# Two transformer layers on one core: layer 1's normalized rows get the projection bias early, in GpSimd's queue, and its last stage is cut into five parts

## The chip, the core and the metric

One Trainium2 chip, one of its cores. A core has a matrix engine (PE; its weight loads are listed apart as PEld), a vector engine (DVE), a scalar engine (ACT), GpSimd (POOL) and a sync engine (SP), which here only issues DMAs. Each engine works through its own queue in order. The metric is device time of the program in microseconds (us), median of several executions.

## The reference

Input: x of 4 x 512 tokens, 512 wide, all in float32. Each of two layers computes `xn = layernorm(x)` and then `x + attention(xn) + experts(xn)`. The change touches the expert part of layer 1:

```python
logits = x @ router_w + router_b            # x is xn here; 8 experts
vals, idx = top_k(logits, 2); w = softmax(vals)
h = x @ expert_w[e] + expert_b[e]           # for the two experts chosen
combined = sum over the two of w * silu(h)
out = combined @ proj_w + proj_b
y = x + out
return norm_w * y / sqrt(mean(y * y) + 1e-6)
```

So the last lines need, for each token, its normalized row plus the projection bias, `x + proj_b`. Layer 1's attention has 16 heads of width 32; its output is added to the same result.

## The kernel before, in words

The 2048 tokens are 16 tiles of 128 rows (`NT = 16`, four to a batch). Layer 0 is done first (to about 1450 us). Its normalization for layer 1 writes the normalized rows to DRAM (`xnd`) and keeps their transpose in SBUF (`xnT`).

**Order of the work.** The kernel is written for a scheduler that traces the program, assumes a time for every instruction, and puts each engine's instructions into a queue by readiness and by their place in the program. `tc.keep_in_program_order(ins)` ties an instruction behind the one traced before it on its engine. The queue that results is fixed: on the chip an instruction whose input is late holds up all that stand behind it.

**Layer 1** runs over 16 groups of four heads (`NG`), each with four key blocks, so 64 steps, `at[0]` to `at[63]`. Each step does the scores (`st`, L1241), their exponential on ACT (`pT`, L1243), the context (`cx`, L1255) and the running sum over keys on DVE (`pS`, L1261). Queries and keys (`qp`), values (`vp`), inverses (`rsum`) and the output projection (`o`, L1324, added to the result on DVE at L1313) are spread over the steps. PSUM has three banks for all `mm` products, and a bank is free again once its reader (mostly DVE) is done.

**Experts among the steps.** After the routing, a list `jobs1` (L1393 to L1434) hangs further work on steps. Within a step the jobs run in the order of the list.
- From step 9: `begin_experts1`, then 36 expert tiles. Each fetches rows (`xr`), one or two sets of weights (`we`, every third into part of `acc`) and a bias (`be`) by indirect DMAs from GpSimd's queue, all in `load` (L478 to L482). A tile is transposed (`trm`, L517) and multiplied (`hp`, L529); its result goes to DRAM (`yd`).
- Step 48: `begin_mixing` gives the experts' SBUF back, opens the pool of the last stage and loads `pw`, `pb`, `nw1`.
- Steps 48 to 63, per token tile n, four parts on successive steps. `mix`: two indirect gathers (`row0`, `row1`, L545), a load of the normalized rows (`xa`, L1354), the first weighting on DVE (L1357), the second with the sum on DVE (L1358), and the bias added on GpSimd (L1359). `turn_mix`: four transposes (`trc`, L1366), ACT's copy (`combT`, L1370). `project_mix`: four products (`po`, L1377), the sum on DVE (L1378), the squares on ACT (`ysq`, L1381), two tiny operations on GpSimd (`yss`, L1382 and L1383). `finish_mix`: scaling on DVE (L1388) and the addition to the result (L1313), then the store.
- Pools of the last stage hold two buffers of each kind.

**At the seam of the layers** (L1436 to L1454) the first values (`vp`), layer 1's last four normalizations (`norm`, `trx`) and the router's logits (`lg`, copied to SBUF as `lr` by ACT, transposed as `trg`) are traced in alternation.

## Time and profile before

| what | value |
|---|---|
| median of 3 runs | 2068.45 us (2067.59 to 2068.87) |
| the profiled execution | 2068.36 us |
| its span, first to last instruction | 2066.3 us |
| PE busy | 2014.5 us, 97% of the span |
| DVE, ACT, POOL busy | 1450.5, 868.2, 753.6 us |
| granted PE clock, mean | 0.996 |
| PE busy in 1560 to 1872 us (expert tiles) | 312.00 of 312.00 us |
| PE busy in 1889 to 2041 us (last stage) | 144.09 of 152.00 us |

The profile is of one execution. The time is 2.06 us more than its span. A line of the timeline gives start, duration, engine, line, operation, output and inputs, shape, count, and in brackets the idle time before it with what ended that time. "Releaser" is the event that came last.

### The profile page before, as it was taken

The page shows a single profiled execution, that of the slowest core. Times are in us where ns is not written, and L with a number is a line of the kernel's source. Part 1 is how long each engine was busy: PE and PEld are TensorE (multiplying, and loading weights), DVE is VectorE, ACT ScalarE, POOL GpSimd, SP SyncE. Part 2 cuts the span into 40 slices and gives each one's busy share as a digit, 9 for nine tenths or more (in the row PEclk, how much of TensorE's full clock was granted, in tenths as well). Part 3 has the DMA queues.
Part 4 walks back from the last instruction along what each step waited for, and adds up shares of the span by engine and source line. Part 5 has one row for each costly group of instructions (what it writes and reads, how often), then busy time and mean ns, then how long its engine had stood idle before and what let it go on. Part 6 is the DMA issues. An engine that isn't in the chain of part 4 may idle for free.

```text
span 2066.3 us, 27983 instructions
## 1 busy us (share of the span) xinstructions
PE 2014.5 (97%) x9130; PEld 1202.9 (58%) x9130; DVE 1450.5 (70%) x3543; ACT 868.2 (42%) x2600; POOL 753.6 (36%) x761
## 2 busy tenths in 40 slices
PE   7999999999999999999999999999999999999998
PEld 4666666666666666666666666666334445445442
DVE  7888967666666766676667778787596555557775
ACT  4554444444444444443444454454243432333332
POOL 4422244443323333344343444353114332332550
PEclk9999999999999999999999999999999999999999
DMA  7111134323332342235443222121317765773551
GB/s 250 68 37 57 42 128 137 123 101 113 139 120 98 118 145 103 95 134 180 182 160 116 72 81 78 42 72 62 120 51 246 262 244 191 262 240 129 155 161 58
DMA packets 98907, 267.23 MB, mean 129 GB/s; under 512 B 14401, under 2 KB 27841, under 8 KB 87489
## 3 DMA queue, kind: packets, MB, share of 16 engines
q0 software_dynamic: 27072, 148.91, 21.2%
q1 hardware_dynamic: 70528, 114.34, 16.3%
q10 hardware_dynamic: 1152, 2.10, 0.3%
q8 instruction: 75, 1.23, 0.2%
q14 instruction: 80, 0.65, 0.1%
HBM read 222.05 MB, written 42.73 MB: 128 GB/s over the span
## 4 chain that ended last, share of the span: by engine, by line
PE 81%; DVE 8%; ACT 3%; POOL 2%; issue 2%; DMA 1%; ACTq 0%; DVEq 0%; POOLq 0%
PE p L675 24%; PE hp_r L529 12%; PE op L842 10%; PE st L767 4%; PE qp L1217 3%; PE st L1241 3%; PE sp L758 3%; PE cx L1255 2%; PE ca L811 2%; PE trm_r L517 2%; PE o L1324 1%; DVE pS L1261 1%; PE trq L695 1%; PE vp L1177 1%; PE cc L814 1%
## 5 line engine op out<-in xcount | busy, mean ns | idle before, releaser
L842 PE MATMUL op<-Wo,cT 128*128 128x512 f32 x512 | 230.4, 598 | 5.3 <-DVE lv L739 2.9
L529 PE MATMUL hp_r<-we_r,xT_r 128*128 128x512 f32 (+1 forms) x592 | 224.7, 596 | 0.0
L481 POOL DMA_INDIRECT xr_r<-xnd,rows_r x72 | 89.4, 1241 | 331.1 <-PE trm_r L517 297.8
L775 POOL TENSOR_TENSOR lT<-lT,lmask 128x512 f32<-128x512 f32 (+1 forms) x128 | 157.9, 1247 | 140.2 <-ACT lT L771 140.0
L675 PE MATMUL p<-wT,x 128*128 128x384 f32 x512 | 179.8, 494 | 0.8 <-DVE wT L119 0.8
L675 PE MATMUL p<-wB,x 128*128 128x384 f32 x512 | 176.2, 488 | 4.0 <-DVE u L731 4.0
L675 PE MATMUL p<-wA,xnT 128*128 128x384 f32 x512 | 173.3, 491 | 0.2 <-DVE u L710 0.2
L842 PEld LDWEIGHTS op<-Wo,cT 128*128 128x128 f32 x512 | 92.0, 190 | 114.7 <-issue 77.9
L575 ACT ACTIVATE sq<-qb 128x128 f32<-128x128 f32 x384 | 118.9, 310 | 93.9 <-DVE qb L724 45.6
L1243 ACT ACTIVATE pT<-st 128x1024 f32<-128x1024 f32 x128 | 123.7, 1014 | 62.7 <-PE st L1241 57.0
L529 PEld LDWEIGHTS hp_r<-we_r,xT_r 128*128 128x128 f32 (+1 forms) x592 | 83.0, 170 | 97.9 <-issue 92.5
L845 DVE TENSOR_TENSOR acc<-acc,op 128x512 f32<-128x512 f32 x128 | 87.4, 685 | 68.9 <-PE op L842 68.5
L675 PEld LDWEIGHTS p<-wB,x 128*128 128x128 f32 x512 | 93.7, 190 | 68.2 <-issue 9.9
L675 PEld LDWEIGHTS p<-wT,x 128*128 128x128 f32 x512 | 94.5, 193 | 63.5 <-issue 6.3
L675 PEld LDWEIGHTS p<-wA,xnT 128*128 128x128 f32 x512 | 95.3, 192 | 60.7 <-issue 2.6
L689 ACT ACTIVATE qb<-qb,ss 128x128 f32<-128x128 f32 x256 | 81.9, 390 | 106.4 <-POOL ss L578 103.3
L519 ACT COPY xT_r<-trm_r 128x512 f32<-128x512 f32 x72 | 41.8, 581 | 197.5 <-PE hp_r L529 187.6
L771 ACT ACTIVATE lT<-st,ss 128x256 f32<-128x256 f32 (+1 forms) x128 | 47.0, 448 | 174.9 <-PE st L767 174.8
L767 PE MATMUL st<-qkT 128*128 128x256 f32 (+1 forms) x512 | 109.0, 353 | 1.5 <-ACT qkT L702 1.5
L545 POOL DMA_INDIRECT row_r<-yd,slot_r x64 | 74.2, 1160 | 95.0 <-DVE row_r L1358 36.7
L767 PEld LDWEIGHTS st<-qkT 128*128 128x128 f32 x512 | 92.0, 191 | 12.8 <-ACT qkT L702 1.7
L578 POOL TENSOR_TENSOR ss<-ss,nhalf 128x6 f32<-128x6 f32 x64 | 96.1, 1501 | 5.3
(360 smaller groups left out, 4330.9 us busy)
## 6 DMA issues: line engine op xcount, KB each, us to landing
x<-xsd SPq DMA_DIRECT2D x112, 256.0 KB, 3.0
yd<-yr_r SPq DMA_DIRECT2D x72, 256.0 KB, 3.5
wA<-in_wA SPq DMA_DIRECT2D x16, 384.0 KB, 3.6
wB<-in_wB SPq DMA_DIRECT2D x16, 384.0 KB, 7.6
xnd<-xn SPq DMA_DIRECT2D x24, 256.0 KB, 2.0
accd<-acc SPq DMA_DIRECT2D x18, 256.0 KB, 2.0
acc<-in_x SPq DMA_DIRECT2D x16, 256.0 KB, 5.8
Wo<-in_Wo SPq DMA_DIRECT2D x8, 512.0 KB, 3.7
```

What stands on the lines that cost most here:

```text
L481: G.indirect_dma_start(out=out, out_offset=None, in_=src, in_offset=at_rows(idx))
L529: PE.matmul(hp[ts(h, m), :], lhsT=xT[:, k, ts(h, m)], rhs=w[:, ts(k, HID)], start=(k == 0), stop=(k == KC - 1))
L545: G.indirect_dma_start(out=x, out_offset=None, in_=self.yd, in_offset=at_rows(self.r.slot[:, k, n : n + 1]))
L575: A.activation(sq, x[:, h, :], AF.Square, accum_out=ss[:, h : h + 1])
L578: pin(G.tensor_tensor(ss, ss, nhalf[:, 0:n], ALU.pow))
L675: PE.matmul(p, lhsT=x[:, k, ts(c, P)], rhs=w[:, k, :], start=(k == 0), stop=(k == 1))
L689: A.activation(x[:, j, :], x[:, j, :], AF.Copy, scale=sq[t][:, j : j + 1])
L767: PE.matmul(st[:, ds((t % 2) * 256, n)], lhsT=qkT[:, HG + h, ts(t, P)], rhs=qkT[:, h, ds(t * P, n)], start=True, stop=True)
L775: G.tensor_tensor(dst, dst, lmask.rearrange("p a w j -> p (a w j)")[:, 0:n], ALU.mult)
L842: PE.matmul(op, lhsT=cT[:, h, ts(t, P)], rhs=wo[:, h, :], start=(h == 0), stop=(h == HG - 1))
L845: V.tensor_tensor(acc[:, n, :], acc[:, n, :], op, ALU.add)
L1243: A.activation(pt[:, ts(pair, 2), :], st, AF.Exp, scale=SCALE1)
```

## The change

In four parts.

1. **Normalized rows plus bias** (`xpd`, a new DRAM array). At step 9 the projection bias is loaded into the row that held layer 1's output bias, no longer needed (`load_bias`). For each of the 16 token tiles, GpSimd's queue loads `xnd`'s rows (step 14 + 2n), and one step later adds the bias and stores the sum to `xpd`. The buffer `xp` is single. These, and all indirect loads of layer 1's experts, are tied to program order.
2. **The last stage in five parts.** `begin_mixing` moves from step 48 to step 47. The gathers become a part of their own (`gather_mix`), one step ahead of the weighting; `row0` gets three buffers, `row1` keeps two. `turn_mix` loads the finished `xpd` rows (four buffers) instead of `mix` loading `xnd` rows, and GpSimd's addition in the last stage is gone. The parts of the first tiles are kept from coming too early, so that tiles 0, 1 and 2 are turned one step later than before; the others on the same steps. The buffer of the squares becomes single.
3. **The first weighting** moves from DVE (a tensor_scalar) to ACT (a Copy activation with the gate as scale). The second, on DVE, is tied to program order for the first four tiles, and so is the last addition of `values7` for the last batch.
4. **At the seam**, the first two normalizations are traced ahead of the first values, and the logits and their transposes come one place earlier.

```diff
+    xpd = dram.tile([T, HID], F32, tag="xpd", name="xpd")
...
-            G.indirect_dma_start(out=out, out_offset=None, in_=src, in_offset=at_rows(idx))
+            pin = tc.keep_in_program_order if self.silu else (lambda x: x)
+            pin(G.indirect_dma_start(out=out, out_offset=None, in_=src, in_offset=at_rows(idx)))
...
+            if b + 1 == B:
+                tc.keep_in_program_order(last_)
...
+    def load_bias():
+        rows["pb"] = rout["wo_b"]
+        nc.sync.dma_start(out=rows["pb"], in_=a["pb"].partition_broadcast(P))
+    def fetch_normalized(n):
+        held["xp", n] = rout["ex1"].pool.tile([P, HID], F32, tag="xp", name=f"xp_{n}", bufs=1)
+        tc.keep_in_program_order(G.dma_start(out=held["xp", n], in_=xnd[ts(n, P), :]))
+    def add_bias(n):
+        x = held.pop(("xp", n))
+        tc.keep_in_program_order(G.tensor_tensor(x, x, rows["pb"], ALU.add))
+        tc.keep_in_program_order(G.dma_start(out=xpd[ts(n, P), :], in_=x))
...
+    def gather_mix(n):
+        held[n] = []
+        for k in range(2):
+            x = rout["mix"].tile([P, HID], F32, tag=f"row{k}", name=f"row{k}_r1_{n}", bufs=3 - k)
+            G.indirect_dma_start(out=x, out_offset=None, in_=yds[1], in_offset=at_rows(r1.slot[:, k, n : n + 1]))
+            held[n].append(x)
     def mix(n):
-        g0, g1 = rout["ex1"].gather(n)
-        x = rout["mix"].tile([P, HID], F32, tag="xr", name=f"xa_{n}")
-        nc.sync.dma_start(out=x, in_=xnd[ts(n, P), :])
-        pin = tc.keep_in_program_order if n < 2 else (lambda x: x)
-        pin(V.tensor_scalar(g0, g0, r1.gate[:, 0, n : n + 1], None, ALU.mult))
-        V.scalar_tensor_tensor(g0, g1, r1.gate[:, 1, n : n + 1], g0, ALU.mult, ALU.add)
-        G.tensor_tensor(x, x, rows["pb"], ALU.add)
+        g0, g1 = held[n]
+        A.activation(g0, g0, AF.Copy, scale=r1.gate[:, 0, n : n + 1])
+        weighed = V.scalar_tensor_tensor(g0, g1, r1.gate[:, 1, n : n + 1], g0, ALU.mult, ALU.add)
+        if n < TC:
+            tc.keep_in_program_order(weighed)
     def turn_mix(n):
-        g0, x = held[n]
+        g0, _ = held[n]
+        x = rout["mix"].tile([P, HID], F32, tag="xr", name=f"xa_{n}", bufs=4)
+        nc.sync.dma_start(out=x, in_=xpd[ts(n, P), :])
...
-    first += 6 + NS * 11 // 12
+    jobs1.append((at[first], load_bias))
+    for n in range(NT):
+        jobs1.append((at[first + 5 + 2 * n], lambda n=n: fetch_normalized(n)))
+        jobs1.append((at[first + 6 + 2 * n], lambda n=n: add_bias(n)))
+    first += 5 + NS * 11 // 12
     jobs1.append((at[first], begin_mixing))
     for n in range(NT):
         here = first + n * 13 // 16
-        for d, f in ((0, mix), (1, turn_mix), (2, project_mix), (3, finish_mix)):
-            jobs1.append((at[here + d], lambda n=n, f=f: f(n)))
+        for d, f in ((0, gather_mix), (1, mix), (2, turn_mix), (3, project_mix), (4, finish_mix)):
+            place = max(here + d, first + 1 + d + (n > 1)) if d else here
+            jobs1.append((at[place], lambda n=n, f=f: f(n)))
...
+    norm = [next_layer(3 * TC + t, rp, bank1) for t in range(2)]
     values(0, 0)
-    norm = [next_layer(3 * TC + t, rp, bank1) for t in range(2)]
     norm[0][0]()
+    turn_ = second_logits(B - 2, rp, bank1)
     values(0, 1)
-    turn_ = second_logits(B - 2, rp, bank1)
+    turn_()
     norm[0][1]()
     norm[1][0]()
     norm.append(next_layer(3 * TC + 2, rp, bank1))
     values(0, 2)
-    turn_()
```

More of the change, by code (lines that the diff above doesn't have):

```diff
@@ L1190, in values7 @@
             V.tensor_tensor(v[b][:, 2:4, h2], p5, u3, ALU.add)
-            V.tensor_tensor(v[b][:, 2:4, h1], product("p3", sv4, block(b, f2, 1)), u2, ALU.add)
+            last_ = V.tensor_tensor(v[b][:, 2:4, h1], product("p3", sv4, block(b, f2, 1)), u2, ALU.add)
+            if b + 1 == B:
+                tc.keep_in_program_order(last_)
     def queries(g, i):
@@ L1344, in begin_mixing @@
         rout["mix"] = scratch.enter_context(tc.tile_pool(name="mix", bufs=2, side="right"))
-        rout["ex1"].pool = rout["mix"]
         load_square(rout["mix"], "pw")
-        for nm in ("pb", "nw1"):
-            rows[nm] = load(rout["mix"], nm, [P, HID], a[nm].partition_broadcast(P))
-    def mix(n):
-        g0, g1 = rout["ex1"].gather(n)
-        x = rout["mix"].tile([P, HID], F32, tag="xr", name=f"xa_{n}")
-        nc.sync.dma_start(out=x, in_=xnd[ts(n, P), :])
-        pin = tc.keep_in_program_order if n < 2 else (lambda x: x)
-        pin(V.tensor_scalar(g0, g0, r1.gate[:, 0, n : n + 1], None, ALU.mult))
-        V.scalar_tensor_tensor(g0, g1, r1.gate[:, 1, n : n + 1], g0, ALU.mult, ALU.add)
-        G.tensor_tensor(x, x, rows["pb"], ALU.add)
-        held[n] = g0, x
+        rows["nw1"] = load(rout["mix"], "nw1", [P, HID], a["nw1"].partition_broadcast(P))
+    def gather_mix(n):
[4 more added lines that the diff above has]
+            held[n].append(x)
+    def mix(n):
+        g0, g1 = held[n]
[3 more added lines that the diff above has]
+            tc.keep_in_program_order(weighed)
     def turn_mix(n):
-        g0, x = held[n]
+        g0, _ = held[n]
+        x = rout["mix"].tile([P, HID], F32, tag="xr", name=f"xa_{n}", bufs=4)
+        nc.sync.dma_start(out=x, in_=xpd[ts(n, P), :])
         tr = bank1("mm", f"trc_{n}")
@@ L1378, in project_mix @@
         V.tensor_tensor(y, y, op, ALU.add)
-        sq = rout["mix"].tile([P, HID], F32, tag="th", name=f"ysq_{n}")
+        sq = rout["mix"].tile([P, HID], F32, tag="th", name=f"ysq_{n}", bufs=1)
         ss = small.tile([P, 1], F32, tag="yss", name=f"yss_{n}")
```

## The prediction, made before the changed kernel was run

> **What bounds the kernel.** I read the page's busy times first. PE is busy 97% of the span, so a change off PE can only win what PE loses. The stages tell where that is.

> ```profile
> PE 2014.5 (97%) x9130; PEld 1202.9 (58%) x9130; DVE 1450.5 (70%) x3543; ACT 868.2 (42%) x2600; POOL 753.6 (36%) x761
> ```
> ```profile
> 1889.00:2041.00 152.00, 144.09 (x618) 64.17 (x616) 110.17 (x154) 55.90 (x96) 70.75 (x74) 0.99 0.42 127
> 1560.00:1872.00 312.00, 312.00 (x1391) 144.04 (x1389) 179.05 (x248) 112.53 (x166) 106.67 (x106) 1.00 0.70 237
> ```

> The lines by window give a stretch, its length and the busy time of PE, PEld, DVE, ACT and POOL, then clock, DMA share and GB/s. Among the expert tiles (1560 to 1872) PE never pauses: work put there is free while its cover lasts, and nothing can be won there. In the last stage PE loses 7.9 us. Where, PE's timeline says:

> ```profile
> 1955.95 3.70 PE L1324 MATMUL o<-woT,cT 128*128 128x512 f32 x8 [0.25 <-DVE xa L1378]
> 1960.12 3.67 PE L1377 MATMUL po<-pw,combT 128*128 128x512 f32 x8 [0.48 <-DVE xa L1378]
> 1968.31 3.53 PE L1217 MATMUL qp<-xnT,wqT 128*128 128x256 f32 x8 [2.01 <-DVE xnT L1313]
> ...
> 2003.29 3.67 PE L1377 MATMUL po<-pw,combT 128*128 128x512 f32 x8 [0.42 <-DVE xa L1378]
> 2011.52 3.67 PE L1377 MATMUL po<-pw,combT 128*128 128x512 f32 x8 [2.05 <-DVE acc L1313]
> 2019.30 3.67 PE L1377 MATMUL po<-pw,combT 128*128 128x512 f32 x8 [0.75 <-DVE xa L1378]
> 2029.50 2.04 PE L1241 MATMUL st<-qk 32*128 32x512 f32 x8 [0.40 <-ACT pT L1243]
> ```

> In all but the last PE waits for DVE to empty a PSUM bank: DVE sets the pace in bursts, though it is busy only 110 of 152 us. Behind the 2.01 us pause the qp products run slowly: the chain of waits gives these 16 products 5.42 us, and 3.65 us elsewhere. The windows show a granted clock of 0.93 in 1960 to 1985, so 0.07 x 25 = 1.75 us of clock are lost there. DVE's and POOL's timelines show why DVE is late:

> ```profile
> 1963.17 0.48 DVE L1357 TENSOR_SCALAR row_r<-row_r,gate_r 128x512 f32<-128x512 f32 x1
> 1963.57 2.29 DVE L1261 TENSOR_TENSOR pS<-pS,pT 128x1024 f32<-128x1024 f32 x1
> ...
> 2007.87 1.76 DVE L1358 SCALAR_TENSOR_TENSOR row_r<-row_r,gate_r,row_r 128x512 f32<-128x512 f32 x1
> ...
> 2017.28 0.49 DVE L1357 TENSOR_SCALAR row_r<-row_r,gate_r 128x512 f32<-128x512 f32 x1 [1.22 <-DMA row_r<-yd,slot_r]
> ```
> ```profile
> 1963.42 1.35 POOL L1359 TENSOR_TENSOR xa<-xa,pb 128x512 f32<-128x512 f32 x1 [1.68 <-DMA xa<-xnd]
> ...
> 2006.83 2.26 POOL L1359 TENSOR_TENSOR xa<-xa,pb 128x512 f32<-128x512 f32 x1 [1.92 <-DVE row_r L1357]
> 2011.18 1.27 POOL L1359 TENSOR_TENSOR xa<-xa,pb 128x512 f32<-128x512 f32 x1 [2.09 <-DMA xa<-xnd]
> 2012.61 1.02 POOL L545 DMA_INDIRECT row_r<-yd,slot_r  x1 [0.16 <-issue]
> ```

> A first weighting takes 0.40 us of a full DVE queue (1963.17 to 1963.57). DVE work that meets GpSimd's addition is drawn out: the `pS` beside the addition at 1963.42 takes 2.29 us, where its neighbours take 1.22, and the second weighting beside the one at 2006.83 takes 1.76, where its median is 0.75 (the addition itself 2.26 instead of 1.28). The addition at 2011.18 waited for its rows, the gather behind it on POOL was issued only at 2012.61, and DVE waited for that gather at 2017.28.

> **The change, part by part**, against the profiled execution (2068.36 us, span 2066.3 plus 2.06; 0.09 under the median).

> *First weighting to ACT, addition out of the last stage* (the gain).
> - The pause before 1968.31. DVE runs from 1961.78 to 1968.26 without a break, and in that run stand one first weighting (0.40) and the drawn-out `pS` (2.29 - 1.22 = 1.07): 1.47 of the 2.01 us go. Bounds 1.0 (the `pS` alone) and 2.0. I take 1.47.
> - The slow clock behind it. The pauses of 0.4 to 0.75 us in the lines above are followed by po at 3.67 us, close to the undisturbed 3.60; so a pause cut to 0.54 should lose nothing. I take 1.75; bounds 0 and 1.75, since the pause of 2.05 us at 2011.52 was not followed by slow products either.
> - 2003 to 2019. The slowed L1358 gives 1.76 - 0.75 = 1.0 back, the weighting 0.40, and the wait for the gather that ends in the 0.75 us pause goes: 2.15. Bounds 1.0 and 3.2 (all three pauses).
> - The end, 2029 to 2041. The score products at 2029.50 lose 0.40 and run 0.9 longer than the usual 1.07 us, because ACT's exponential stands behind squares that wait for DVE. DVE stood 1.22 us for a gather in the line at 2017.28; being that much earlier it gives 1.2 here too. The last products (pauses of 0.53 and 0.68 us; 0.97 and 1.15 us over their usual times) I leave: they hang on the last tile's own chain. Bounds 0 and 4.6.
> - The pauses of 0.25 and 0.48 us: nothing taken; bounds 0 and 1.0.

> Sum 1.47 + 1.75 + 2.15 + 1.2 = 6.57, say 6.6 us.

> *ACT's side.* 16 activations of 128x512 at 0.63 us (the squares' row) are 10 us beside 96 idle ones, at no cost by themselves. But a Copy whose gather is late now holds up exponentials. DVE waited 3.1 us in total for gathers in front of L1357; that wait moves to ACT at worst, so the bounds are 0 and 3.1. The gathers start a step (9.5 us) ahead of the weighting and land in 4.1 us (median; 7.8 at most), so I take a quarter, 0.8.

> *Bias among the expert tiles.* Per tile one plain load, one addition, one plain store on POOL. The addition is 1.28 to 2.26 us. No plain DMA from POOL is in this trace: an issue is 0.32 us on SP, an indirect one on POOL 0.95, at most 2.1; I take 0.95 as the same queue. With 0.30 us between issues that is 1.25 + 1.28 + 1.25 = 3.8 us of POOL, 61 us in all; POOL rises from 107 to 168 of 312 us. Its queue waits for PE's releases in gaps of 2 to 4 us, so most of this falls into idle time. DMA: 16 x 512 KB more, 8.4 on 74 MB in that stage, share 0.70 to 0.78. What is queued behind: the next rows and weights. The tightest weights I found were issued at 1605.69 and used at 1617.66; they land in 6.2 us, so 5.8 us of cover. The addition waits for rows loaded a step before (9.5 us; such loads land in 4.6), the next load for a store a step before: no new wait. Cost 0; the price without cover is the second rival.

> *Moving the start and the three first turns.* Gathers began at 1876.53, soon after the last `yd` store (SP's queue lists the last two from 1864.21 to 1873.84; in that stage they land in 5.5 us); a step earlier cannot hurry that. The later turns of tiles 0 to 2 shift PE work between steps that are full. 0; bounds 0 and 1.0 lost. The 16 loads of the last stage come from `xpd` instead of `xnd`, equal in size; with four buffers SP waits less for a free one.

> *The seam.* PE pauses 0.83 us at 1458.28 (for ACT's copy of the logits), 0.68 and 0.80 us at the next two. With the logits ahead of the second values that copy is hidden. But two of three banks are held by values until their bias lands (DVE 1461.35), so the transposed logits and tile 12 share the third, and a DVE queue that waits for the bias would hold tile 12 until 1462: 3.8 us. Bounds 1.5 won and 3.8 lost; I take 0, nearest to the small pauses.

> **Sum**: 6.6 - 0.8 = 5.8; 2068.36 - 5.8 = **2062.6 us**.

> [...] On the clock, the trace shows a 2.01 us pause followed by half speed. [...]

> **Rivals.**
> 1. *The pauses move instead of closing.* DVE's breaks of 1.8 to 3.1 us before L1388, for the chain squares, `yss`, scaling, stay (29.5 us in all), and the queues are planned anew. Then only the drawn-out operations give something back: 1.0 + 1.0, and the clock or not. 2068.36 - 2.0 = 2066.4 us. For it: no part of that chain is shortened. Against: both large pauses have the weighting and the addition in the DVE run before them.
> 2. *Slower: POOL's one fixed order starves the experts.* All fetches are now tied behind additions. If an addition's rows or a store land late in the busy queue (DMA share over 0.7), POOL stands still, and weights follow late. It decides from 5.8 us of extra hold in front of a tight set. Price: 3.8 us of work plus a wait of 6 (a landing there) less 5.8 is 4 us, at the 4 of 8 half tiles that meet such a pass, 16 us: 2062.6 + 16 = 2079 us. Against: half of POOL's time is idle.

> **Chances.** Forecast (faster by over 0.2%, which is about what a measurement of this kernel can tell, 4.1 us) 0.60; first rival 0.26, within 0.2%; second rival, with a badly planned seam, 0.14, slower. Range 2056 to 2073: below, most of the upper bounds together (gain 12); above, all lower bounds (1.0 + 0 + 1.0 won, 3.1 + 1.0 + 3.8 lost: 2074.3), shortened by 1 as they hardly meet. It leaves out most of the slow case.

> **What would show it.** Right: no L1359 in the last stage, no `pS` or L1358 drawn out, gathers not behind an addition, granted clock 1.00 in 1960 to 1985, PE busy over 148 of the 152 us, and 312 of 312 among the experts. Wrong: pauses of `hp` for `we` (second rival); exponentials behind Copies that wait for gathers; a PE pause over 2 us between 1449 and 1470; or pauses before bank releases that add up to 7 us again.

## The result, and the profile after

The changed kernel takes 2074.11 us (median of 11 runs, 2072.36 to 2079.12), the kernel before 2068.45: a ratio of 1.0032, 95% interval 1.0025 to 1.0040. It is slower by 5.2 to 8.3 us, where 5.8 us faster was forecast, and lies outside the range. The profiled execution is the median one (2074.11 us, span 2072.2, against 2068.36 and 2066.3).

The busy line and two windows of the changed kernel (stretch, length, PE, PEld, DVE, ACT, POOL, clock, DMA share, GB/s):

```profile
PE 2013.5 (97%) x9130; PEld 1204.5 (58%) x9130; DVE 1446.2 (70%) x3527; ACT 878.7 (42%) x2616; POOL 771.0 (37%) x793
```
```profile
1560.00:1872.00 312.00, 312.00 (x1380) 144.74 (x1380) 182.12 (x241) 112.44 (x166) 151.30 (x155) 1.00 0.76 263
1895.00:2047.00 152.00, 145.91 (x625) 65.03 (x626) 105.38 (x146) 65.62 (x111) 50.15 (x59) 0.98 0.39 123
```

Among the expert tiles nothing is lost: PE is busy 312 of 312 us though POOL went from 107 to 151 and the DMA share from 0.70 to 0.76. DVE and POOL are relieved in the last stage, as meant. The loss stands in PE's timeline at two places that the prediction had priced at 0 and at 0.8 us (the number in brackets is the idle time before the line and what ended it):

```profile
1558.56 0.88 PE L520 MATMUL trm_r<-ident,xr_r 128*128 128x128 f32 x4 [2.63 <-DMA xr_r<-xnd,rows_r]
1559.24 5.08 PE L532 MATMUL hp_r<-we_r,xT_r 128*128 128x512 f32 x8
...
1896.85 5.32 PE L1330 MATMUL o<-woT,cT 128*128 128x512 f32 x8 [6.54 <-DVE v L1190]
...
1918.13 2.04 PE L1247 MATMUL st<-qk 32*128 32x512 f32 x8 [1.44 <-ACT pT L1249]
...
1952.88 3.70 PE L1402 MATMUL po<-pw,combT 128*128 128x512 f32 x8 [1.08 <-ACT rsum L1280]
```

PE waits 2.63 us for the rows of the third expert tile, and 6.54 us for a bank that DVE empties at the handover from the experts to the last stage. Behind both the products run slowly (5.08 and 5.32 us; 3.60 undisturbed), at a granted clock of 0.50 from 1558.81 to 1562.22 us and from 1893.31 to 1900.14. The old pauses of 2.01 and 2.05 us are gone. In the kernel before PE passed both places without a pause:

```profile
1557.83 0.66 PE L517 MATMUL trm_r<-ident,xr_r 128*128 128x128 f32 x4
1887.75 3.60 PE L1324 MATMUL o<-woT,cT 128*128 128x512 f32 x8
```

To put a place to each microsecond I set landmarks that every kernel has: ScalarE's row sums of the exponentials (16 in layer 1) at 1553.69, 1591.67, 1865.17, 1900.06 and 2041.65 us of the kernel before, and the span's end. The table gives by how much each stretch grew against the kernel before. The executions differ by -1.4 to +0.9 us already at 80 us, ahead of all that was edited, so the first column holds that scatter beside the seam.

| kernel (profiled execution) | up to 1554 | experts' start | expert tiles | handover | last stage | after it | span |
|---|---|---|---|---|---|---|---|
| changed | -1.97 | **+4.37** | 0.00 | **+8.42** | **-7.51** | **+2.6** | +5.9 |
| changed, again | -1.52 | +3.86 | +0.67 | +9.63 | -7.31 | +2.7 | +8.0 |
| Copies pinned | -0.09 | +3.67 | +0.63 | 0.00 | -7.50 | +2.7 | -0.6 |
| weights first | -0.29 | -0.34 | 0.00 | +8.60 | -7.21 | +2.6 | +3.4 |
| DMAs by SyncE | -1.70 | +2.30 | 0.00 | +10.21 | -6.91 | 0.0 | +3.9 |
| all three | -0.60 | -0.36 | -0.01 | 0.00 | -5.24 | +0.1 | -6.1 |

(Sums are rounded; the last column is the span less 2066.3.) The last stage won 7.5 us, more than the 5.8 forecast; three losses of together 15.4 us outweigh it.

**At the handover** ScalarE's timeline of the changed kernel shows what holds DVE's bank:

```profile
1887.63 0.72 ACT L1380 ACTIVATE row_r<-row_r,gate_r 128x512 f32<-128x512 f32 x1 [10.65 <-DMA xa<-xpd]
1890.13 0.72 ACT L1380 ACTIVATE row_r<-row_r,gate_r 128x512 f32<-128x512 f32 x1 [1.77 <-DMA row_r<-yd,slot_r]
1892.17 0.72 ACT L1380 ACTIVATE row_r<-row_r,gate_r 128x512 f32<-128x512 f32 x1 [1.33 <-DMA row_r<-yd,slot_r]
1892.80 1.92 ACT L1249 ACTIVATE pT<-st 128x1024 f32<-128x1024 f32 x2
```
```profile
1893.84 2.36 DVE L1267 TENSOR_TENSOR pS<-pS,pT 128x1024 f32<-128x1024 f32 x2 [9.51 <-ACT pT L1249]
1896.11 0.68 DVE L1190 TENSOR_TENSOR v<-xnT,vp 128x512 f32<-128x512 f32 x1
```

Only the second weightings of the first four tiles are held in program order, not the Copies (L1380). The planner put three Copies ahead of the exponential of the 47th step. In the kernel before, that one waited only for its scores:

```profile
1881.63 1.94 ACT L1243 ACTIVATE pT<-st 128x1024 f32<-128x1024 f32 x2 [7.05 <-PE st L1241]
```

The Copies' gathers are issued from 1879.62 to 1884.71, five in a row, and land 7.6 us later (median; the last at 1892.15). That is slow only against the stage's median of 4.1 us: the first four gathers of the kernel before took 7.4 (median) as well. So the exponential waits, behind it DVE's sum and behind that the sum that empties PE's bank. (The release named in the first line, `xa`, can't be the cause: the Copy doesn't read it. Its own gather, issued at 1879.62, landed by the median near 1887.2.)

### The profile page after: what moved, and what is told of

Read it like the earlier page. It is cut to its first block, busy times and chain, and to the rows that moved or that the text cites. A ratio compares the mean times of both kernels' runs of the same rounds, so it can differ in the third digit from the quotient of the medians.

```text
span 2072.2 us, 27992 instructions
## 1 busy us (share of the span) xinstructions
PE 2013.5 (97%) x9130; PEld 1204.5 (58%) x9130; DVE 1446.2 (70%) x3527; ACT 878.7 (42%) x2616; POOL 771.0 (37%) x793
## 4 chain that ended last, share of the span: by engine, by line
PE 80%; DVE 7%; ACT 4%; DMA 2%; POOL 2%; issue 2%; ACTq 0%; DVEq 0%; SPq 0%; POOLq 0%
PE p L678 23%; PE hp_r L532 12%; PE op L845 10%; PE st L770 4%; PE st L1247 3%; PE qp L1223 3%; PE sp L761 2%; PE cx L1261 2%; PE o L1330 2%; PE ca L814 2%; PE trm_r L520 2%; PE po L1402 1%; PE trq L698 1%; DMA row_r<-yd,slot_r 1%; PE cc L817 1%
## 5 line engine op out<-in xcount | busy, mean ns | idle before, releaser
L580 POOL TENSOR_SCALAR ss<-ss 128x6 f32<-128x6 f32 x64 | 31.4, 490 | 170.3 <-ACT sq L578 170.1
```

## The experiments

All times were compared with the kernel before on the same chip; its medians there were 2068.0 to 2068.3 us.

**1. Copies pinned.** The changed kernel with:

```
-        A.activation(g0, g0, AF.Copy, scale=r1.gate[:, 0, n : n + 1])
+        scaled = A.activation(g0, g0, AF.Copy, scale=r1.gate[:, 0, n : n + 1])
+        if n < TC:
+            tc.keep_in_program_order(scaled)
```

> The changed kernel with one thing more: the Copies of the first four tiles (the first weighting on ScalarE, L1380) are held in program order. Theory (the changed kernel loses its 8.4 us at the 47th and 48th step because three Copies stand in ScalarE's queue ahead of step 47's exponential and wait there for gathers): the exponential runs near 1882 to 1884 instead of 1892.80, the 6.54 us pause of PE before the output products of 1896.85 goes, they run in 3.6 to 3.7 us instead of 5.32, and the time falls by about 8 us from 2074.1 to some 2066. Rival (the five gathers come late in themselves, because they are issued behind one another on GpSimd, and whatever waits for them holds the stage, VectorE's second weightings in program order above all): the pause is found again at another instruction and the time stays over 2072.

Measured: 2068.43 us, ratio 1.0000 (0.9991 to 1.0009). The exponential runs at 1885.85, 4.2 us behind its old place (the loss up to there, 3.7 of it at the experts' start), and PE doesn't pause. PE's timeline of this kernel:

```profile
1891.97 3.60 PE L1330 MATMUL o<-woT,cT 128*128 128x512 f32 x8
...
1911.53 2.04 PE L1247 MATMUL st<-qk 32*128 32x512 f32 x8 [1.44 <-ACT pT L1249]
```

The handover costs 0.00 instead of 8.42 us with the same gathers at the same place: the queue order, not the gathers, was the loss. The rival falls. The time fell by 5.7 us by the medians, less than the 8 expected; of the 8.4 us the start's scatter took back 1.9 between the two profiled executions (first column of the table).

**2. Weights first.** The changed kernel with the fetch of the third weights moved up:

```
     jobs1.append((at[first], begin_experts1))
+    jobs1.append((at[first], lambda: rout["ex1"].fetch_weights(2)))
...
-    jobs1.append((at[first], lambda: rout["ex1"].fetch_weights(2)))
```

> The changed kernel with the third set of the experts' weights asked for later in the program's order only in one respect: its fetch is written right behind the beginning of the expert stage, where the kernel before also issued it (near 1508), and no longer between the second and third rows. Theory (the 4.4 us at the experts' start come from the fixed order of GpSimd's fetches, in which the third weights stand ahead of the third rows, so that the rows land at 1558.5 and PE pauses 2.63 us, with a slow clock behind it): the pause before L520 goes, the first hidden products take 3.6 us instead of 5.08, and the time falls by about 4 us to some 2070. Rival (the rows are late because GpSimd's queue and the DMA engines are crowded by the bias work, whatever the order): PE still pauses over 2 us near 1558 and the time stays at 2074.

Measured: 2071.54 us, ratio 1.0018 (1.0009 to 1.0027). GpSimd's queue in the changed kernel (first fence), and the third weights' fetch, which comes ahead of all the others here (second fence) as it did in the kernel before (third fence):

```profile
1550.32 0.94 POOL L484 DMA_INDIRECT acc<-in_ewm,wrow_r  x1 [0.30 <-DMA xr_r<-xnd,rows_r]
1551.56 0.95 POOL L484 DMA_INDIRECT xr_r<-xnd,rows_r  x1 [0.31 <-issue]
```
```profile
1507.73 2.43 POOL L484 DMA_INDIRECT acc<-in_ewm,wrow_r  x1 [37.20 <-DVE row_f_r L425]
```
```profile
1508.36 2.43 POOL L481 DMA_INDIRECT acc<-in_ewm,wrow_r  x1 [37.13 <-DVE row_f_r L423]
```

The pause near 1558 is gone and the experts' start costs -0.34 instead of +4.37 us. The time fell by 0.0014, some 3 us where 4 were expected, with the handover still there: the theory held.

**3. DMAs by SyncE.** The changed kernel with the bias rows' loads and stores on SyncE, the additions left on GpSimd:

```
-        tc.keep_in_program_order(G.dma_start(out=held["xp", n], in_=xnd[ts(n, P), :]))
+        nc.sync.dma_start(out=held["xp", n], in_=xnd[ts(n, P), :])
...
-        tc.keep_in_program_order(G.dma_start(out=xpd[ts(n, P), :], in_=x))
+        nc.sync.dma_start(out=xpd[ts(n, P), :], in_=x)
```

> The changed kernel with the 16 loads of normalized rows and the 16 stores of rows with the bias issued from SyncE; the additions stay on GpSimd, in program order. Theory (the 2.5 us that the changed kernel loses after VectorE's last addition are GpSimd's last drain, 7.26 us instead of 4.65, and it is longer because plain DMAs went through GpSimd's queue): the drain is near 4.7 us again and the time falls by about 2.5 us to 2071.5. Rival (the drain has another cause, such as the number of indirect DMAs or the last stores): the drain stays at 7.3 us and the time at 2074. If SyncE's queue is the tighter one, PE pauses among the expert tiles and the time rises above 2075.

Measured: 2072.59 us, ratio 1.0027 (1.0016 to 1.0038), an interval that overlaps the changed kernel's. The trace decides: GpSimd's last instruction, a drain, takes 4.65 us as before instead of 7.26, and the stretch behind the last stage has its old length again. In this execution the clock moved two other stretches the opposite way: the handover cost 1.8 us more (slow for 10.24 us instead of 6.83), the experts' start 2.1 less (no slow clock behind a pause of 2.62 us). PE doesn't pause among the expert tiles.

**4. Pins only.** The kernel before with nothing but the pinned fetches:

```
-            G.indirect_dma_start(out=out, out_offset=None, in_=src, in_offset=at_rows(idx))
+            pin = tc.keep_in_program_order if self.silu else (lambda x: x)
+            pin(G.indirect_dma_start(out=out, out_offset=None, in_=src, in_offset=at_rows(idx)))
```

> The kernel before with one part of the change alone: layer 1's fetches of rows, weights and biases of the experts are held in program order on GpSimd. Nothing else is changed, and no bias work is in the queue. Theory (this order alone delays the third rows at the experts' start): PE pauses 2 to 3 us near 1558 before the turned rows of the third tile, and the time rises by 2.6 to 4.4 us, from 2068.4 to 2071 or 2073. Rival (the order alone is harmless, the 4.4 us came from the additions and loads that stand in the queue): no such pause, and the time stays within 1 us of 2068.4.

Measured: 2071.65 us, ratio 1.0015 (1.0006 to 1.0024). PE's timeline of this kernel:

```profile
1560.39 0.63 PE L518 MATMUL trm_r<-ident,xr_r 128*128 128x128 f32 x4 [1.75 <-DMA xr_r<-xnd,rows_r]
1560.86 3.60 PE L530 MATMUL hp_r<-we_r,xT_r 128*128 128x512 f32 x8
```

The order alone makes the pause, without any bias work in the queue, though a shorter one than the 2 to 3 us expected. Here the products behind it run at full speed (3.60 us), and the stretch costs 1.56 us; the last stage adds 0.6. (The span grew by 3.4, of which 1.1 stands in the scatter before 1554.)

**5. All three together**, edits 1 to 3.

> The changed kernel with all three repairs: the first four Copies in program order, the third weights asked for at the beginning of the expert stage, the loads and stores of the bias rows issued from SyncE. Theory (three separate losses: Copies in front of an exponential, the order of GpSimd's first fetches, GpSimd's longer last drain; the last stage itself is shorter): the gains add up, 2068.4 with the Copies repaired, less 2.7 to 4.4 for the weights, less 2.2 for the drain and SyncE, gives 2061.8 to 2063.5, below the kernel before. Rival (the losses are one shift in the program's phase that moves on to another place, as part of the second repair's gain did): a new pause of over 2 us turns up and the time stays over 2066.

Measured: **2060.45 us, ratio 0.9957 (0.9943 to 0.9971)**, faster than both kernels. The three losses are gone at once (last row of the table) and none turned up elsewhere. It came out a little below the expected range.

**6. The same kernel twice more**, to see the clock.

> The kernel with the three repairs once more, unchanged, for one more profiled execution. In the first one a pause of 1.45 us near 1906 was followed by two stretches of 3.41 us at half clock (6.83 us; the score products behind it took 2.81 us, the output products 5.36), while the kernel with the Copies alone repaired had the same pause of 1.44 us with products at full clock behind it (2.04 and 3.70). Theory (the clock is judged over stretches of a fixed grid of 3.413 us that does not start anew with the kernel, so the same pause costs clock or not by where it falls): the pause of 1.45 us is there again, and in some execution the products behind it run at full speed. Rival (this kernel's work around the pause always brings the half clock): 2.8 and 5.4 us again in each execution.

> As the run before it: the same kernel again, a third profiled execution. Theory (grid): among the three executions the products behind the 1.45 us pause differ, 2.0 and 3.7 us where the clock was kept, 2.8 and 5.4 where it was halved. Rival (fixed by the kernel's own work): the same as in the first.

Measured: 2058.56 and 2062.14 us. PE's timeline of the first execution (experiment 5, 2062.25 us), then of the second:

```profile
1906.35 2.81 PE L1247 MATMUL st<-qk 32*128 32x512 f32 x8 [1.45 <-ACT pT L1249]
1909.09 1.94 PE L1261 MATMUL cx<-pT,v 128*32 128x512 f32 x8
1910.95 5.36 PE L1330 MATMUL o<-woT,cT 128*128 128x512 f32 x8
```
```profile
1905.10 2.04 PE L1247 MATMUL st<-qk 32*128 32x512 f32 x8 [1.44 <-ACT pT L1249]
1907.07 1.06 PE L1261 MATMUL cx<-pT,v 128*32 128x512 f32 x8
1908.07 3.70 PE L1330 MATMUL o<-woT,cT 128*128 128x512 f32 x8
```

The third (2062.14 us) is like the first: 2.99, 1.94, 5.02. One kernel, one pause, and the three groups behind it take 10.1 us or 6.8: the clock is lost or kept from execution to execution, so the rival falls. The theory's grid fits: the pause began 0.82 us behind an edge of the grid (the line between two stretches of 3.413 us) in the first execution and 1.31 in the third, where the clock was lost, and 1.47 in the second, where it was kept (the last section has all pauses). Counted from the first instruction, the edge ahead of the pause lies at 1904.08 us in the first execution (1906.35 - 1.45 - 0.82) and at 1902.19 in the second (1905.10 - 1.44 - 1.47): 1.89 us apart, no multiple of 3.413, so the grid does not begin with the program's first instruction. By the landmarks the last stage is 2.3 us shorter where it was kept (-7.57 against -5.24); another 1.3 of the 3.7 us between the two times are the start's scatter.

**7. First weighting on VectorE again**, on top of the three repairs:

```
-        scaled = A.activation(g0, g0, AF.Copy, scale=r1.gate[:, 0, n : n + 1])
+        scaled = V.tensor_scalar(g0, g0, r1.gate[:, 0, n : n + 1], None, ALU.mult)
```

> The kernel with the three repairs, with the first weighting back on VectorE (in program order for the first four tiles, as the Copies were). Theory (VectorE's queue is full in front of PE's waits, so 16 operations of 0.40 to 0.48 us taken out of it are worth about 1 to 2 us): the time rises by 1 to 3 us against the kernel with the three repairs, and PE waits for banks that VectorE empties again. Rival (the gain of the last stage comes from the addition's removal and from the gathers that run a step ahead; the weighting's engine is of no account, since VectorE has some 45 of 152 us idle): within 1 us of it.

Measured: 2061.49 us, ratio 0.9964 (0.9951 to 0.9978). PE's pauses between 1900 and 2050 add up to 5.77 us instead of 3.43, and it waits for DVE's banks again (1.06 us before `qp`, 1.15 before `po`), as the theory has it. By the times it is unclear: 1.0 us by the medians, and the two intervals overlap. The traces can be compared where neither had a slow stretch in the last stage, this one and the second of experiment 6: by the landmarks the stage is 1.75 us longer here (-5.82 against -7.57), PE's pauses 5.77 us against 4.07. That is one pair of executions, and inside the theory's range.

**8. Addition back in the last stage**, on top of the three repairs: the jobs `fetch_normalized` and `add_bias` are left out, and `mix` has

```
+        x = rout["mix"].tile([P, HID], F32, tag="xr", name=f"xa_{n}", bufs=4)
+        nc.sync.dma_start(out=x, in_=xnd[ts(n, P), :])
+        G.tensor_tensor(x, x, rows["pb"], ALU.add)
+        held[n] = g0, x
```

> The kernel with the three repairs, with the projection bias added in the last stage again by GpSimd (rows loaded from the normalized rows in the weighting's step), and no bias work among the expert tiles. The five parts and the weighting on ScalarE stay. Theory (the addition draws VectorE's operations out and so makes the pauses): pS sums or second weightings of 1.7 to 2.3 us show again beside it, and the time rises by 2 to 4 us against the kernel with the three repairs. Rival (what made PE wait was the gather that was issued behind a late addition and used in the same step; with the gathers a step ahead the addition harms little): within 1 us of it, although the drawn-out operations are there.

Measured: 2065.31 us, ratio 0.9985 (0.9976 to 0.9994), 4.9 us over the kernel with the three repairs. Its PE pauses add up to 7.75 us (7.82 in the kernel before, 3.43 without the addition). GpSimd, VectorE and PE of this kernel at one of them:

```profile
1966.31 1.69 POOL L1388 TENSOR_TENSOR xa<-xa,wo_b 128x512 f32<-128x512 f32 x1 [2.08 <-DMA xa<-xnd]
```
```profile
1966.79 1.76 DVE L1383 SCALAR_TENSOR_TENSOR row_r<-row_r,gate_r,row_r 128x512 f32<-128x512 f32 x1
```
```profile
1970.34 1.99 PE L1223 MATMUL qp<-xnT,wqT 128*128 128x256 f32 x8 [1.54 <-DVE xnT L1319]
```

The weighting beside the addition takes 1.76 us (0.75 elsewhere), and PE waits for DVE soon after, at the place of the old 2.01 us pause. The addition costs 4.9 us though the gathers run a step ahead here: the rival falls. How it costs them is shown in part only. Of the 7.75 us of pauses 1.45 stand before the score products with and without the addition, and 2.68 (1.58 and 1.10) end with ScalarE's row sums, not with DVE. And with the addition back the last stage is still 2.4 us shorter than in the kernel before, each with one slow stretch of 3.41 us, so the addition isn't the whole gain.

**9. One plain DMA.** The kernel before, with the projection bias loaded from GpSimd's queue instead of SyncE's:

```
-        for nm in ("pb", "nw1"):
-            rows[nm] = load(rout["mix"], nm, [P, HID], a[nm].partition_broadcast(P))
+        rows["nw1"] = load(rout["mix"], "nw1", [P, HID], a["nw1"].partition_broadcast(P))
+        rows["pb"] = rout["mix"].tile([P, HID], F32, tag="pb", name="pb", bufs=1)
+        G.dma_start(out=rows["pb"], in_=a["pb"].partition_broadcast(P))
```

> The kernel before with one difference: the projection bias, a single load at the start of the last stage, is issued as a plain DMA from GpSimd instead of SyncE. Theory (one plain DMA in GpSimd's queue is enough to lengthen the last drain, whatever their number): the drain lasts 7.3 us instead of 4.65 and the time rises by 2.6 us to 2070.7. Rival (each of the 32 plain DMAs costs its share, 2.61/32 = 0.08 us): the drain lasts 4.7 us and the time stays at 2068.1.

Measured: 2067.88 us, ratio 0.9999 (0.9990 to 1.0008). The last drain takes 4.727 us instead of 4.651: 0.076 for one plain DMA, and (7.264 - 4.651) / 32 = 0.082 for each of the change's 32. The rival was right: the drain grows with the number of plain DMAs. My theory, that one is enough, fell.

**10. Seam only.** The kernel before with the edits of the seam (the first two normalizations ahead of the first values, the second logits ahead of the second values, the last value addition pinned).

> The kernel before with the seam alone changed: the second logits ahead of the second values, and the last value addition held in program order. Theory (the traces of all kernels with the whole change show PE some 1.2 us earlier behind the seam, its 0.83 us pause for ScalarE's copy of the logits gone): the pause goes and the time falls by about 1.2 us to 2067. Rival (a bank held by the values gives it back, or the 1.2 us are lost further on, in the wait for the experts' lists or rows): time unchanged, and the experts' first products start when they did.

Measured: 2066.48 us, ratio 0.9994 (0.9985 to 1.0003): in the expected direction, not told from no change. In the trace the 0.83 us pause is 0.45 and one of 0.80 is gone; 1.0 of the 2.1 us by which it is ahead at 1554 stand in the start's scatter, so some 1.1 us are the seam's, and they stay to the end.

**11. The changed kernel again.**

> The changed kernel again, unchanged, on the chip of these runs. Theory (three Copies ahead of an exponential, a fixed order of fetches, a longer drain): 2073 to 2076 us, 6.5 us without PE before the output products at the 47th step, the rows late by 2.6 us at the experts' start, a drain of 7.26 us. Rival (the loss at the handover hangs on when the gathers happen to land): a pause of another length, under 5 or over 8 us.

Measured: 2075.05 us, ratio 1.0035 (1.0021 to 1.0049); pauses of 2.47 us at the experts' start and 6.38 at the handover, a drain of 7.26. The loss isn't an accident of one execution.

## Why the prediction was wrong, step by step

- **What bounds the kernel; the last stage.** Right in the main. The gain taken was 6.6 us; the stretch won 7.5 with the new waits included. Some of that is luck with the clock: it was kept behind the pause of 1.44 us here, and where it was lost behind the same pause for 6.83 us (all three repairs, first and third execution) the stage won 5.2 and 5.3. The drawn-out sums and weightings are gone (L1381 takes 0.74 us in the mean, the old L1358 took 0.87), and the clock in 1960 to 1985 is 1.00. Experiment 8 shows that the addition is most of it (4.9 us with three repairs); the first weighting is worth 1.0 us by unclear times and 1.75 by one pair of traces.
- **"ACT's side", 0.8 us, bounds 0 and 3.1.** This step failed, and it is the largest loss: 8.4 us, more than the whole forecast gain. It isn't the only one: without it (experiment 1) the kernel takes 2068.43 us, no faster than before, so the two losses below eat the gain as well. "That wait moves to ACT at worst" took it for granted that a Copy stands where the weighting stood. The old weightings of the first two tiles were pinned behind the work of their step; the Copies were not pinned, and the planner placed three of them ahead of an exponential on which PE's bank hangs. The bound was a sum of DVE's waits in the old order, and no bound in another. The landing time (4.1 us) was a median over the stage; the gathers at its start, which these Copies wait for, took 7.6 us in the changed kernel and 7.4 already in the profile that the prediction read. I named this mechanism ("exponentials behind Copies that wait for gathers"), and priced it at a quarter of the wrong sum.
- **"Moving the start and the three first turns", 0, at most 1.0 lost.** Wrong for the same reason: it is the place where the Copies met the exponential.
- **"Bias among the expert tiles", 0.** Right for the work: POOL is busy 44.6 us more in that stage (the forecast's 61 holds gaps of 0.30 us; without them it is 51, and a plain issue took 0.58 us, not 0.95), DMA share 0.76 (0.78 forecast), PE without a pause. But the step left out the order: I listed what is queued behind the additions, not which fetch the pins put in front of which. The third weights, which the planner had hoisted to 1508.36, went ahead of the third rows, and that costs 4.4 us here, 2.3 where the clock was kept behind the pause (experiment 3) and 1.6 with the pins alone (experiment 4). The second rival had the kind of cause (POOL's fixed order), another place (the middle of the experts) and another mechanism (additions that land late): neither its landing wait nor its 16 us was seen.
- **The seam, 0, bounds 1.5 won and 3.8 lost.** Some 1.1 us won in experiment 10's trace, 0.7 to 1.8 in the others with this edit (the lead at 1554 less that at 80 us), in the bounds; the times don't tell it from none.
- **The end of the program.** No term. 32 plain DMAs in GpSimd's queue lengthen its last instruction, a drain, which ends 0.8 us before the span does: 2.6 us.
- **The slow clock, 1.75 us.** The place was right, the reasoning not: "a pause cut to 0.54 should lose nothing" treats the length of a pause alone as what decides. Experiment 6 has the same 1.45 us with and without: the clock was lost where the pause began 0.82 and 1.31 us behind an edge of the grid, and kept where it began 1.47 us behind one (last section).

The sum by what was measured: 2066.3 - 2.0 (seam and scatter) + 4.4 + 8.4 - 7.5 + 2.6 = 2072.2 us of span. The range failed with the first step: its upper end was the sum of bounds of which one was no bound, and two losses of together 7.0 us had neither a cost nor a bound in it.

Among the expert tiles the issues of the plain DMAs took GpSimd little time. The groups of POOL in the changed kernel, 1560 to 1872 (count | busy us, mean ns | idle before):

```profile
L1360 POOL TENSOR_TENSOR xp<-xp,wo_b 128x512 f32<-128x512 f32 x16 | 20.6, 1287 | 5.7 <-DMA xp<-xnd 5.4
...
L1356 POOL DMA_DIRECT2D xp<-xnd x16 | 9.5, 592 | 5.9 <-DMA xpd<-xp 5.9
L1361 POOL DMA_DIRECT2D xpd<-xp x16 | 9.2, 577 | 4.7 <-POOL xp L1360 4.7
```

The 32 issues take 18.7 us, 0.59 us for a load and 0.58 for a store in the mean, where the prediction took 0.95.

## What to carry to other kernels

When an operation moves to another engine, its price is not its duration but what stands behind it there in the planned order (here 8.42 us behind Copies of 0.72 us each): find the first critical instruction behind each moved one, and pin it behind that one when its data may be late. When a queue is pinned, write down which instruction had been hoisted and is no longer (here the third weights: 1.6 to 4.4 us). And look at the last instruction of the span: what ends the program may grow with what was queued long before (here the drain, from 4.65 to 7.26 us).
